# Two of the three layer-2 projections as seven block products, the ones products later, and the check of the sums in two parts

## The chip, the cores and the metric

The kernel runs on one core of one Trainium2 chip. The metric is the time of one execution on the device in microseconds (us). The core works with engines that run side by side and wait for each other through semaphores: TensorE (PE in the profile; its weight loads are PEld), VectorE (DVE), ScalarE (ACT), GpSimd (POOL) and the queue that starts most transfers (SP). A tile framework orders the instructions of each engine by its own schedule, so the order on an engine is not always that of the source.

## The reference

Eight images of 512 channels and 32 x 32 = 1024 pixels pass through four layers in float32, each layer on the output of the one before:

```python
# layer 0: 1x1 convolutions f, g, h (512 -> 64), z = f.T g per image, attn = z / sigma_max(z), x = x + Wv (attn h)
# layer 1, an attention over the 1024 pixels of an image with 512 channels:
h = _group_norm(x, gamma, beta).reshape(B, C, N)
q, k, v = wq h + bq, wk h + bk, wv h + bv
attn = softmax(q.T k * 512 ** -0.5)
x = x + wp (attn v) + bp
# layer 2, an attention with 128 channels:
proj = jnp.einsum('oc,ncq->noq', W_w, xf) + W_b[None, :, None]     # W_w: 384 x 512
t, p, g = jnp.split(proj, 3, axis=1)                                # 128 rows each
s = softmax(jnp.einsum('ncq,nck->nqk', t, p) * 128 ** -0.5, axis=2)
att = jnp.einsum('nqv,ncv->ncq', s, g)
x = x + batchnorm(Z_w att)
# layer 3: binarised 1x1 convolution, batchnorm, residual, PReLU
```

The changed part is t and p of layer 2: two matrices of 128 x 1024 per image, each a product of 128 x 512 weights with the image.

## The kernel before

A first part (about 210 us) loads and prepares weights, runs layer 0's convolutions and starts its singular values. Then `fast` runs once per image for layers 1 to 3; the singular values of later images (`chore`, `chain`) and the next image's products (`fill`) are put between the products of the current one. Tiles: P = 128, N = 1024, HF = 512, C = 512, CC = 4 channel blocks, NH = 2 halves of the pixels, NT = 8 and NTH = 4 pixel blocks, B = 8 images.

Large products are made from seven block products instead of eight (Strassen's scheme in Winograd's form). `sums_of` makes S1 to S4 from the blocks of the left matrix, `differences_of` T1 to T4 from those of the right one, and `seven` runs the products and adds them up. `product_of` gives `term`: two matmuls of 512 columns (or four of 256) for one block product.

```python
    def differences_of(b, more):

        b11, b12, b21, b22 = b
        t1, t2, t4 = more
        tt = nc.vector.tensor_tensor
        tt(t1, b12, b11, ALU.subtract)
        tt(t2, b22, t1, ALU.subtract)
        tt(b12, b22, b12, ALU.subtract)
        tt(t4, b21, t2, ALU.subtract)
        return {"B11": b11, "B21": b21, "B22": b22, "T1": t1, "T2": t2, "T3": b12, "T4": t4}

    def seven(term, c11, c12, c21, c22, b1=None, b2=None, exp=None, then=None):
        ...   # move: ScalarE PSUM -> SBUF with bias; plus: VectorE dst = PSUM (+ bias) + u
        pa, va = term(None, "A11", "B11", True, False)
        nc.scalar.copy(c21, va)
        yield
        _, vb = term(None, "S2", "T2", True, True)
        plus(vb, None, c21, c21)
        yield
        pd, vd = term(None, "S3", "T3", True, False)
        plus(vd, None, c21, c22)
        yield
        pc, vc = term(None, "S1", "T1", True, False)
        move(c12, vc, b2)
        nc.gpsimd.tensor_tensor(c22, c22, c12, ALU.add)
        yield
        term(pa, "A12", "B21", False, True)      # accumulates into the bank of A11 B11
        ...                                      # c11 <- va
        yield
        term(pc, "S4", "B22", False, True)
        plus(vc, b1, c21, c12)
        yield
        term(pd, "A22", "T4", False, True)
        plus(vd, b2, c21, c21)
        ...
```

`make_v` runs `seven` twice and `scores1` four times per image. Layer 2's t, p and g were made directly, and the row sums of the exponentials are turned into their inverses by `inverse_sums`, whose matmuls have a matrix of ones as weights:

```python
    def project2(env, xt, fill=lambda h: None):

        big = env["big"]
        tpg = big.tile([P, 3, N], F32, tag="us", name="tpg")
        tt, pt = tpg[:, 0:1, :], tpg[:, 1:2, :]
        gt = tpg[:, 2, :].rearrange("p (t c) -> p t c", c=P)
        for h in reversed(range(NH)):
            for i, dst in enumerate((tt, pt)):
                ps = bank()
                for cc in range(CC):
                    mm(
                        out=ps,
                        lhsT=sbw["tpg"][:, cc, bass.ts(i, P)],
                        rhs=xt[:, cc, half(h)],
                        start=cc == 0,
                        stop=cc == CC - 1,
                    )
                evacuate(i, dst[:, 0, half(h)], ps, col("L2_conv_W_b", i))
                fill(h)
            ps = bank().rearrange("p (t c) -> p t c", c=P)
            for i in range(4):
                for cc in range(CC):
                    mm(
                        out=ps[:, i, :],
                        lhsT=xt[:, cc, bass.ts(4 * h + i, P)],
                        rhs=sbw["tpg"][:, cc, 2 * P : 3 * P],
                        start=cc == 0,
                        stop=cc == CC - 1,
                    )
            nc.vector.tensor_tensor(
                gt[:, bass.ts(h, 4), :], ps, bg_row.unsqueeze(1).to_broadcast([P, 4, P]), ALU.add
            )
            fill(h)
        return tt, pt, gt

    def inverse_sums(env, esum, row):
        ps = bank()
        for h in range(NH):
            mm(out=ps[side(h), :], lhsT=ones2[:, 0:MID], rhs=esum[:, half(h)], start=True, stop=True)
        r = env["small"].tile([P, HF], F32, tag="rsum", name="rsum", bufs=1)
        nc.vector.reciprocal(r, ps)
        full = env["small"].tile([P, NH, HF], F32, tag="rfull", name="rfull", bufs=1)
        ...   # four DMAs: r to both halves of the partitions of full; two DMAs: rows of r to guard
        return full
```

The end of layer 1 (`values1`) updates the image `xt` in place on GpSimd, a half of a channel block at a time:

```python
        def scaled(dst, oc, h):               # inside values1
            nc.vector.tensor_tensor(dst, dst, r[:, h, :], ALU.mult)
            xs = xt[:, oc, half(h)]
            nc.gpsimd.tensor_tensor(xs, xs, dst, ALU.add)
        ...
        for i in range(2):
            group(pc[i], a12, e22, i, False, True)
            d = temp(i)
            tt(d, pc[i], u[i], ALU.add)
            scaled(d, i, 1)
            yield
        pd = [bank(), bank()]
        for i in range(2):
            group(pd[i], a21, e12, i, True, False)
            tt(p5[i], p5[i], u[i], ALU.add)
            tt(p5[i], pd[i], p5[i], ALU.add)
            scaled(p5[i], 2 + i, 1)
            yield
        for i in range(2):
            group(pd[i], a22, e21, i, False, True)
            tt(u[i], pd[i], u[i], ALU.add)
            scaled(u[i], 2 + i, 0)
            yield
```

One image, and the check of the row sums at the end of the last one (its result decides whether a general path runs after the fast one; with these inputs it does not):

```python
    def fast(env, n, hb, ua):
        ...                                   # scores1: seven products for each of 4 row blocks
        esum = es.pop()
        vt = env["big"].tile([P, NT, C], F32, tag="uv", name="vt")
        r = None
        for _ in make_v(hb, vt):              # 2 x seven products
            if r is None:
                r = inverse_sums(env, esum, n)
            chore(2)
        ...
        for k, _ in enumerate(values1(env, xt, vt, es, r, scratch)):   # 14 groups of 4 products
            ...                               # k == 5: h and its differences for the next image
        ...
        def fill(k=1):                        # one of the next image's u products
            for _ in range(k):
                next(steps, None)

        tt, pt, gt = project2(env, xt, lambda h: fill(1 - h))
        es, esum = scores2(env, pt, tt, lambda t: fill(t % 2))
        ...
        fill()
        values2(0, range(0, 1))
        r = inverse_sums(env, esum, B + n)
        values2(0, range(1, NTH))
        att = values2(0, range(NTH, NT))
        values2(1, range(0, NTH))
        close2(xt, att, 0)
        att = values2(1, range(NTH, NT))
        fill()
        for _ in leave(env, xt, dst, [0], signs):
            fill()
        close2(xt, att, 1)
        fill(2)
        for _ in steps:
            pass
        rest3.append(leave(env, xt, dst, [1], signs))
        if not more:                          # the last image
            verdict.append(count_bad(env))
            for _ in rest3.pop():
                pass

    def count_bad(env):
        g = 2 * B * 4
        ...                                   # tiles fine, other, nbad in the pool late
        nc.vector.tensor_scalar(fine, guard, 1.0 / GUARD, None, ALU.is_gt)
        nc.vector.tensor_scalar(other, guard, GUARD, None, ALU.is_lt)
        nc.vector.tensor_tensor(fine, fine, other, ALU.mult)
        ...                                   # twice: compare halves of guard, multiply into fine
        nc.vector.tensor_reduce(nbad, fine.rearrange("p h n -> p (h n)"), AX.X, ALU.min)
        nc.vector.tensor_scalar(nbad, nbad, -1.0, 1.0, ALU.mult, ALU.add)
        ps = bank()
        mm(out=ps[0:1, 0:1], lhsT=nbad, rhs=ones2[0:g, 0:1], start=True, stop=True)
        nc.vector.tensor_copy(bad, ps[0:1, 0:1])
        return nc.values_load(bad, min_val=0, max_val=P)
```

Of the kernel before, what the change touches and what calls it, by code (L numbers as in the profile page):

```python
# [83 lines left out]
def kernel(  # L84
# [527 lines left out]
    def project2(env, xt, fill=lambda h: None):  # L612

        big = env["big"]
        tpg = big.tile([P, 3, N], F32, tag="us", name="tpg")
        tt, pt = tpg[:, 0:1, :], tpg[:, 1:2, :]
        gt = tpg[:, 2, :].rearrange("p (t c) -> p t c", c=P)
        for h in reversed(range(NH)):
            for i, dst in enumerate((tt, pt)):
                ps = bank()  # L620
                for cc in range(CC):
                    mm(  # L622
                        out=ps,
                        lhsT=sbw["tpg"][:, cc, bass.ts(i, P)],
                        rhs=xt[:, cc, half(h)],
                        start=cc == 0,
                        stop=cc == CC - 1,
                    )
# [90 lines left out]
    def count_bad(env):  # L719
# [4 lines left out]
        fine = late.tile([g, NH, P], F32, tag="fine", name="fine")  # L724
        other = late.tile([g, NH, P], F32, tag="other", name="other")
# [14 lines left out]
        nc.vector.tensor_copy(bad, ps[0:1, 0:1])  # L740
        return nc.values_load(bad, min_val=0, max_val=P)
# [72 lines left out]
    def fast(env, n, hb, ua):  # L814
# [52 lines left out]
        tt, pt, gt = project2(env, xt, lambda h: fill(1 - h))  # L867
# [23 lines left out]
        values2(0, range(0, 1))  # L891
        r = inverse_sums(env, esum, B + n)
        values2(0, range(1, NTH))
# [3 lines left out]
        att = values2(1, range(NTH, NT))  # L897
        fill()
# [449 lines left out]
    with ExitStack() as main:  # L1348
# [9 lines left out]
        ua = got[0]  # L1358
        for n in range(B):
            hb, ua = fast(env, n, hb, ua)  # L1360
# [31 lines left out]
    def general(env, xt, b, dst):  # L1392
# [55 lines left out]
        tt, pt, gt = project2(env, xt)  # L1448
# [23 lines left out]
    with tc.If(verdict[0] > 0):  # L1472
        with (
            ExitStack() as stack,
            tc.tile_pool(name="gbig", bufs=1) as big,
            tc.tile_pool(name="gepool", bufs=2) as epool,
# [5 lines left out]
            for a in weights.values():  # L1482
                nc.vector.tensor_tensor(a["S3"], a["A11"], a["S3"], ALU.subtract)
# [45 lines left out]
```

## Time and profile before

Three executions took 1985.38, 1987.02 and 1988.73 us, median 1987.02. The profiled one has a span of 1984.6 us and a mean granted TensorE clock of 0.992.

| engine | busy us | share of the span | instructions |
|---|---|---|---|
| PE (matmuls) | 1929.4 | 97% | 6262 |
| PEld (weight loads) | 993.9 | 50% | 6262 |
| DVE | 1104.4 | 56% | 1807 |
| ACT | 507.8 | 26% | 803 |
| POOL | 203.9 | 10% | 168 |

A float32 matmul shows as two records in the trace, so counts of matmuls are twice those of the source: `project2`'s t and p have 16 matmuls of 512 columns per image, 128 in all, and 256 records. Records overlap in a pipeline: one lasts 592 ns for 512 columns, but the next one starts 429 ns after it when nothing holds it up. So a stream of matmuls is best measured from start to start. The timeline gives for each engine start, duration, line, tiles, count, and in brackets the idle time before it and who ended it. The groups by line and the waits give the same by kind, summed over the run.

### The profile page before, as it was taken

To read this page: it belongs to the slowest core of one execution; us is meant where nothing else is said; L and a number is where in the kernel's file an instruction comes from. 1 tells how busy PE (TensorE), PEld (TensorE's weight loads), DVE (VectorE), ACT (ScalarE), POOL (GpSimd) and SP (SyncE) were. 2 spreads that over 40 slices of the span, in tenths; PEclk is the share of its full clock that TensorE was granted. 3 is DMA by queue.
4 is the path that set the end of the run, shared out by engine and by line. 5 is a ranking of instruction groups with operands and counts; after the bars stand their busy time and mean duration, and the time that the engine had idled before them with its cause. 6 is when DMAs were issued, how large, how long until landed. Compare 5 with 4: busy or idle time off the path is not lost.

```text
span 1984.6 us, 16624 instructions
## 1 busy us (share of the span) xinstructions
PE 1929.4 (97%) x6262; PEld 993.9 (50%) x6262; DVE 1104.4 (56%) x1807; ACT 507.8 (26%) x803; POOL 203.9 (10%) x168
## 2 busy tenths in 40 slices
PE   8999899999999999999999999999999999999997
PEld 2377346544565446454455446444645445544653
DVE  3235577337863586536752677238653775266526
ACT  2132122034220432024211341034202421134114
POOL 1000101100011000200111002100120011101110
PEclk9989999999999999999999999999999999999999
DMA  8320000002000020001100120002000110010001
GB/s 332 128 75 1 6 6 12 1 11 85 11 6 0 22 74 17 0 0 57 45 11 1 32 69 11 0 11 85 11 0 1 54 44 9 0 32 22 11 1 55
DMA packets 26712, 66.99 MB, mean 34 GB/s; under 512 B 3760, under 2 KB 4016, under 8 KB 25984
## 3 DMA queue, kind: packets, MB, share of 16 engines
q1 hardware_dynamic: 25968, 65.09, 9.7%
q8 instruction: 51, 0.84, 0.2%
q0 software_dynamic: 224, 0.33, 0.1%
q10 hardware_dynamic: 432, 0.43, 0.1%
q14 instruction: 37, 0.30, 0.1%
HBM read 38.51 MB, written 18.87 MB: 29 GB/s over the span
## 4 chain that ended last, share of the span: by engine, by line
PE 92%; DVE 5%; ACT 2%; POOL 1%; issue 1%; DMA 0%; DVEq 0%; ACTq 0%
PE bank L370 36%; PE bank L537 19%; PE bank L875 6%; PE bank L622 6%; PE bank L755 6%; PE bank L1122 4%; PE bank L634 3%; PE bank L651 3%; PE bank L393 2%; PE bank L671 1%; PE bank L926 1%; PE bank L1232 1%; PE wide L1178 1%; PE bank L927 1%; PE bank L776 1%; DVE e L327 1%
## 5 line engine op out<-in xcount | busy, mean ns | idle before, releaser
L537 PE MATMUL bank<-e,vt 128*128 128x512 f32 x768 | 334.0, 593 | 0.0
L537 PEld LDWEIGHTS bank<-e,vt 128*128 128x128 f32 x768 | 145.0, 190 | 175.3 <-issue 171.7
L370 PE MATMUL bank<-ut,h 128*128 128x512 f32 x384 | 183.3, 598 | 4.7 <-ACT e L332 4.7
L370 PE MATMUL bank<-us,hs 128*128 128x512 f32 x256 | 121.3, 596 | 0.5 <-DVE us L299 0.5
L327 DVE TENSOR_TENSOR e<-bank,e 128x512 f32<-128x512 f32 x128 | 87.8, 686 | 61.1 <-PE bank L370 59.8
L875 PE MATMUL bank<-e,tpg 128*128 128x512 f32 x256 | 114.6, 595 | 0.0
L755 PE MATMUL bank<-tpg 128*128 128x512 f32 x256 | 114.6, 592 | 0.0
L370 PEld LDWEIGHTS bank<-ut,h 128*128 128x128 f32 x384 | 70.6, 190 | 87.7 <-issue 73.5
L622 PE MATMUL bank<-xt,tpg 128*128 128x512 f32 x256 | 113.6, 592 | 0.0
L762 ACT ACTIVATE e<-bank 128x512 f32<-128x512 f32 x128 | 76.4, 597 | 96.1 <-PE bank L755 96.1
L370 PE MATMUL bank<-wo,h 128*128 128x256 f32 x384 | 92.1, 383 | 5.6 <-ACT vt L332 5.6
L370 PE MATMUL bank<-h,wu 128*128 128x512 f32 x192 | 92.0, 602 | 4.7 <-DVE h L443 4.1
L327 DVE TENSOR_TENSOR vt<-bank,vt 128x512 f32<-128x512 f32 x64 | 43.9, 686 | 83.6 <-PE bank L370 82.7
L767 DVE TENSOR_TENSOR esum<-esum,e 128x1024 f32<-128x1024 f32 x48 | 58.8, 1225 | 54.9 <-ACT e L762 54.9
L342 POOL TENSOR_TENSOR e<-e 128x512 f32<-128x512 f32 x32 | 41.6, 1300 | 432.2 <-ACT e L321 361.3
L370 PEld LDWEIGHTS bank<-wo,h 128*128 128x128 f32 x384 | 71.6, 190 | 18.2 <-ACT vt L332 8.8
L875 PEld LDWEIGHTS bank<-e,tpg 128*128 128x128 f32 x256 | 48.0, 190 | 63.9 <-issue 63.9
L755 PEld LDWEIGHTS bank<-tpg 128*128 128x128 f32 x256 | 48.6, 190 | 60.7 <-issue 58.6
L342 POOL TENSOR_TENSOR ut<-ut 128x512 f32<-128x512 f32 x16 | 21.7, 1359 | 532.2 <-ACT ut L323 532.2
L622 PEld LDWEIGHTS bank<-xt,tpg 128*128 128x128 f32 x256 | 47.9, 190 | 56.4 <-issue 55.0
L370 PEld LDWEIGHTS bank<-us,hs 128*128 128x128 f32 x256 | 47.3, 190 | 57.5 <-issue 51.4
L661 ACT ACTIVATE sg<-xt,rb 128x512 f16<-128x512 f32 x64 | 43.7, 717 | 103.6 <-DVE xt L653 100.9
(304 smaller groups left out, 2974.3 us busy)
## 6 DMA issues: line engine op xcount, KB each, us to landing
xt<-in_x SPq DMA_DIRECT2D x56, 512.0 KB
out<-both SPq DMA_DIRECT2D x64, 256.0 KB
rfull<-rsum SPq DMA_DIRECT2D x64, 128.0 KB
f_dram<-f SPq DMA_DIRECT2D x8, 256.0 KB
fb<-f_dram SPq DMA_DIRECT2D x8, 256.0 KB
w<-in_w SPq DMA_DIRECT2D x1, 1024.0 KB
q<-in_w_q SPq DMA_DIRECT2D x1, 1024.0 KB
k<-in_w_k SPq DMA_DIRECT2D x1, 1024.0 KB
```

The source lines that it names most:

```text
L327: nc.vector.tensor_tensor(dst, ps, u, ALU.add)
L342: nc.gpsimd.tensor_tensor(c22, c22, c12, ALU.add)
L370: mm(out=ps[:, q * w : (q + 1) * w], lhsT=lt(ka, kb, q, k), rhs=rhs(ka, kb, q, k), start=first and q == 0 and k == 0, stop=last and k == 1 ...
L537: mm(out=ps, lhsT=a[:, t, bass.ts(r_, P)], rhs=e[t], start=first and t == 0, stop=last and t == NTH - 1, skip_group_check=True,)
L622: mm(out=ps, lhsT=sbw["tpg"][:, cc, bass.ts(i, P)], rhs=xt[:, cc, half(h)], start=cc == 0, stop=cc == CC - 1,)
L634: mm(out=ps[:, i, :], lhsT=xt[:, cc, bass.ts(4 * h + i, P)], rhs=sbw["tpg"][:, cc, 2 * P : 3 * P], start=cc == 0, stop=cc == CC - 1,)
L651: mm(out=ps, lhsT=sbw["z"][:, bass.ts(oc, P)], rhs=att, start=True, stop=True)
L755: mm(out=ps, lhsT=pt[:, 0, bass.ts(t, P)], rhs=tt[:, 0, half(h)], start=True, stop=True,)
L762: nc.scalar.activation(e[:, half(h)], ps, AF.Exp, scale=float(P) ** -0.5)
L767: nc.vector.tensor_tensor(esum, esum, e, ALU.add)
L875: mm(out=banks[h], lhsT=gt[:, t, :], rhs=es[t][:, half(h)], start=t == 0, stop=t == NT - 1,)
L1122: mm(out=banks[i][side(h), :], lhsT=w0[i][:, cc, :], rhs=xt[:, cc, half(h)], start=cc == 0, stop=cc == CC - 1,)
```

## The change

Three things change.

1. t and p become one product of 256 x 512 weights with the 512 x 1024 image, split in 2 x 2 blocks of 128 x 256 and 256 x 512, and made by `seven`. The weights' sums are formed once (`sp`, three tiles of 128 x 256, and one block of the weights overwritten). The differences are formed per image on VectorE from `xt`, each 128 x 1024, into four tiles of the pool `e` that also holds the exponentials; `xt` itself must stay, so `differences_of` takes a fourth tile. g stays direct and now comes after all of t and p; the next image's products are called at the last three steps.
2. The ones products of layer 1 come after the fourth product of `make_v` instead of after the first, and those of layer 2 after two of the value matmuls instead of one.
3. `count_bad` is a generator: its VectorE part is called before the output of the last image's first half, its matmul and the load of the result while the second half is put out. Two of its tiles move to another pool.

The aim is fewer matmuls, and ones products that do not hold up TensorE while the sums are still being formed. The diff (the general path's part, which does not run here, is cut, as are two changes of pool):

```diff
@@ -304,13 +304,13 @@
     def differences_of(b, more):
 
         b11, b12, b21, b22 = b
-        t1, t2, t4 = more
+        t1, t2, t4, t3 = (list(more) + [b12])[:4]
         tt = nc.vector.tensor_tensor
         tt(t1, b12, b11, ALU.subtract)
         tt(t2, b22, t1, ALU.subtract)
-        tt(b12, b22, b12, ALU.subtract)
+        tt(t3, b22, b12, ALU.subtract)
         tt(t4, b21, t2, ALU.subtract)
-        return {"B11": b11, "B21": b21, "B22": b22, "T1": t1, "T2": t2, "T3": b12, "T4": t4}
+        return {"B11": b11, "B21": b21, "B22": b22, "T1": t1, "T2": t2, "T3": t3, "T4": t4}
 
     def seven(term, c11, c12, c21, c22, b1=None, b2=None, exp=None, then=None):
 
@@ -609,25 +609,29 @@
             scaled(u[i], 2 + i, 0)
             yield
 
-    def project2(env, xt, fill=lambda h: None):
+    def project2(env, xt, made):
+
 
         big = env["big"]
         tpg = big.tile([P, 3, N], F32, tag="us", name="tpg")
         tt, pt = tpg[:, 0:1, :], tpg[:, 1:2, :]
         gt = tpg[:, 2, :].rearrange("p (t c) -> p t c", c=P)
+        wa = weights["tp"]
+        xb = differences_of(
+            [xt[:, chunks[k], half(n)] for k in range(2) for n in range(2)],
+            [env["e"].tile([P, 2, HF], F32, tag="e", name="xd") for i in range(4)],
+        )
+        term = product_of(lambda a, b, q, k: wa[a][:, k, :], lambda a, b, q, k: xb[b][:, k, :])
+        yield from seven(
+            term,
+            tt[:, 0, half(0)],
+            tt[:, 0, half(1)],
+            pt[:, 0, half(0)],
+            pt[:, 0, half(1)],
+            col("L2_conv_W_b", 0),
+            col("L2_conv_W_b", 1),
+        )
         for h in reversed(range(NH)):
-            for i, dst in enumerate((tt, pt)):
-                ps = bank()
-                for cc in range(CC):
-                    mm(
-                        out=ps,
-                        lhsT=sbw["tpg"][:, cc, bass.ts(i, P)],
-                        rhs=xt[:, cc, half(h)],
-                        start=cc == 0,
-                        stop=cc == CC - 1,
-                    )
-                evacuate(i, dst[:, 0, half(h)], ps, col("L2_conv_W_b", i))
-                fill(h)
             ps = bank().rearrange("p (t c) -> p t c", c=P)
             for i in range(4):
                 for cc in range(CC):
@@ -641,8 +645,8 @@
             nc.vector.tensor_tensor(
                 gt[:, bass.ts(h, 4), :], ps, bg_row.unsqueeze(1).to_broadcast([P, 4, P]), ALU.add
             )
-            fill(h)
-        return tt, pt, gt
+            yield
+        made.extend((tt, pt, gt))
 
     def close2(xt, att, h):
 
...
@@ -735,10 +739,12 @@
             nc.vector.tensor_tensor(fine[one, h, :], fine[one, h, :], other[one, h, :], ALU.mult)
         nc.vector.tensor_reduce(nbad, fine.rearrange("p h n -> p (h n)"), AX.X, ALU.min)
         nc.vector.tensor_scalar(nbad, nbad, -1.0, 1.0, ALU.mult, ALU.add)
+        yield
         ps = bank()
         mm(out=ps[0:1, 0:1], lhsT=nbad, rhs=ones2[0:g, 0:1], start=True, stop=True)
         nc.vector.tensor_copy(bad, ps[0:1, 0:1])
-        return nc.values_load(bad, min_val=0, max_val=P)
+        verdict.append(nc.values_load(bad, min_val=0, max_val=P))
+        yield
 
     def channels(ap):
         return ap.rearrange("(cc p) n -> p cc n", p=P)
@@ -841,9 +847,8 @@
             pass
         esum = es.pop()
         vt = env["big"].tile([P, NT, C], F32, tag="uv", name="vt")
-        r = None
-        for _ in make_v(hb, vt):
-            if r is None:
+        for k, _ in enumerate(make_v(hb, vt)):
+            if k == 3:
                 r = inverse_sums(env, esum, n)
             chore(2)
         scratch = env["big"].tile([P, 3, N], F32, tag="us", name="scratch")
@@ -864,7 +869,10 @@
             for _ in range(k):
                 next(steps, None)
 
-        tt, pt, gt = project2(env, xt, lambda h: fill(1 - h))
+        made = []
+        for k, _ in enumerate(project2(env, xt, made)):
+            fill(k > 5)
+        tt, pt, gt = made
         es, esum = scores2(env, pt, tt, lambda t: fill(t % 2))
         banks, r = [None, None], None
 
@@ -888,13 +896,15 @@
 
         dst = channels(out[b])
         fill()
-        values2(0, range(0, 1))
+        values2(0, range(0, 2))
         r = inverse_sums(env, esum, B + n)
-        values2(0, range(1, NTH))
+        values2(0, range(2, NTH))
         att = values2(0, range(NTH, NT))
         values2(1, range(0, NTH))
         close2(xt, att, 0)
         att = values2(1, range(NTH, NT))
+        count = iter(()) if more else count_bad(env)
+        next(count, None)
         fill()
         for _ in leave(env, xt, dst, [0], signs):
             fill()
@@ -904,9 +914,8 @@
             pass
         rest3.append(leave(env, xt, dst, [1], signs))
         if not more:
-            verdict.append(count_bad(env))
             for _ in rest3.pop():
-                pass
+                next(count, None)
 
         return hb, got[0] if more else None
 
@@ -1356,6 +1365,9 @@
         for _ in make_u(env, hb, got):
             pass
         ua = got[0]
+        sp = late.tile([P, 3, 2, P], F32, tag="sp", name="sp")
+        tp = quarters_of(sbw["tpg"], chunks, [slice(0, P), slice(P, 2 * P)])
+        weights["tp"] = sums_of(tp, [sp[:, i] for i in range(3)])
         for n in range(B):
             hb, ua = fast(env, n, hb, ua)
 
...
...
```

More of the change, by code (lines that the diff above doesn't have):

```diff
@@ L723, in count_bad @@
         g = 2 * B * 4
-        fine = late.tile([g, NH, P], F32, tag="fine", name="fine")
-        other = late.tile([g, NH, P], F32, tag="other", name="other")
+        fine = env["small"].tile([g, NH, P], F32, tag="half_a", name="fine")
+        other = env["small"].tile([g, NH, P], F32, tag="half_b", name="other")
         nbad = late.tile([g, 1], F32, tag="nbad", name="nbad")
@@ L1447, in general @@
         attention(env, rows1, float(C) ** -0.5, apply1)
-        tt, pt, gt = project2(env, xt)
+        made = []
+        for _ in project2(env, xt, made):
+            pass
+        tt, pt, gt = made
         def rows2(ps, t):
@@ L1475 @@
             tc.tile_pool(name="gbig", bufs=1) as big,
-            tc.tile_pool(name="gepool", bufs=2) as epool,
+            tc.tile_pool(name="gepool", bufs=4) as epool,
             tc.tile_pool(name="gsmall", bufs=2) as small,
@@ L1480 @@
             psum_pools(stack, 2, 4)
-            for a in weights.values():
+            for a in (weights["u"], weights["o"]):
                 nc.vector.tensor_tensor(a["S3"], a["A11"], a["S3"], ALU.subtract)
```

## The prediction

> **What bounds the kernel now.** I read the page's busy times first, then its chain that ended last, then the waits of TensorE, then the timeline of TensorE around the two places that the change touches, and last the timeline of the tail.
>
> ```profile
> PE 1929.4 (97%) x6262; PEld 993.9 (50%) x6262; DVE 1104.4 (56%) x1807; ACT 507.8 (26%) x803; POOL 203.9 (10%) x168
> ...
> PE 92%; DVE 5%; ACT 2%; POOL 1%; issue 1%; DMA 0%; DVEq 0%; ACTq 0%
> ```
>
> TensorE carries 92% of the chain that ended last. So a matmul removed is time gained nearly one for one, and work added to VectorE (56% busy) costs only where TensorE, or the short tail after it, waits for it. Where TensorE waits already is in the waits of that engine (line, releaser, us in total, times, longest):
>
> ```profile
> PE bank L776 <- DVE esum L517: 6.2, 7, 1.5
> PE bank L370 <- ACT vt L332: 5.6, 8, 0.7
> ...
> PE bank L370 <- DVE h L443: 4.1, 1, 4.1
> ```
>
> The first two belong together. L776 is the ones product of layer 1, which waits for the last addition to the row sums; the other is a product of `make_v`. The timeline of TensorE at one image (start, duration, what) shows both:
>
> ```profile
> 982.00 1.97 PE L370 MATMUL bank<-wo,h 128*128 128x256 f32 x8
> 984.64 1.99 PE L370 MATMUL bank<-wo,h 128*128 128x256 f32 x8 [0.67 <-ACT vt L332]
> 987.09 1.08 PE L776 MATMUL bank<-esum,ones 128*64 128x512 f32 x4 [0.46 <-DVE esum L517]
> 988.10 1.99 PE L370 MATMUL bank<-so,hs 128*128 128x256 f32 x8
> 989.93 1.89 PE L370 MATMUL bank<-wo,h 128*128 128x256 f32 x8
> 991.66 1.89 PE L370 MATMUL bank<-so,hs 128*128 128x256 f32 x8
> ```
>
> A block product undisturbed takes 1.72 us from start to start (991.66 - 989.93 = 1.73). The first one here takes 2.64, the second 2.45. The order explains it: the framework put A12 B21 directly after A11 B11, because the ones product stood next in the source and its operand wasn't there. A12 B21 accumulates into the bank that ScalarE has first to copy out, so it waits, and then the ones product waits for its sums all the same.
>
> The t and p products and their surroundings, from the timeline of TensorE and of VectorE and GpSimd at the same image:
>
> ```profile
> 1029.60 27.63 PE L537 MATMUL bank<-e,vt 128*128 128x512 f32 x64
> 1057.07 7.03 PE L622 MATMUL bank<-xt,tpg 128*128 128x512 f32 x16
> 1063.94 3.73 PE L634 MATMUL bank<-tpg,xt 128*128 128x128 f32 x32
> ...
> 1057.27 0.69 DVE L608 TENSOR_TENSOR o_a<-bank,o_a 128x512 f32<-128x512 f32 x1 [2.01 <-PE bank L537]
> ...
> 1048.47 1.27 POOL L550 TENSOR_TENSOR xt<-xt,o_b 128x512 f32<-128x512 f32 x1 [2.10 <-DVE o_b L548]
> 1051.90 1.27 POOL L550 TENSOR_TENSOR xt<-xt,o_b 128x512 f32<-128x512 f32 x1 [2.17 <-DVE o_b L548]
> 1055.34 1.27 POOL L550 TENSOR_TENSOR xt<-xt,o_a 128x512 f32<-128x512 f32 x1 [2.17 <-DVE o_a L548]
> 1058.77 1.27 POOL L550 TENSOR_TENSOR xt<-xt,o_a 128x512 f32<-128x512 f32 x1 [2.17 <-DVE o_a L548]
> ```
>
> Half of t and p (8 matmuls, 16 records) runs from 1057.07 to 1063.94, with no wait: 6.87 / 8 = 0.859 us a matmul. VectorE is idle two thirds of this stretch. The four POOL lines are the last updates of `xt`: channel blocks 2 and 3 of the right half, then of the left half, the last one done at 1060.04, 3 us after the products of layer 2 have begun.
>
> [...]the GpSimd addition of L576 takes 1262 ns at best and 2248 in the median, beside VectorE's L581[...].
>
> **The change part by part.**
>
> *Fewer matmuls.* Per image t and p take 2 x 2 x 4 = 16 matmuls of 512 columns; seven block products of two matmuls take 14. Two times 0.859 us times 8 images is 13.7 us less, all of it on the chain. g keeps its 32 short matmuls; the number of products of the next image that fill in stays three.
>
> *Do the new operands come in time?* The four differences take 1.22 us each on VectorE, 4.9 us per image. I follow them by hand at the image shown. T1 needs the left and right halves of blocks 0 and 1 and a buffer whose exponentials are read by the first matmuls after 1046.8; it can run from 1048.4 to 1049.6[...]. T2 and T3 need the addition that ends at 1053.2 (or 1053.8): T2 at 54.5 to 55.0, T3 at 55.7 to 56.2. That pushes L608 and its multiplication at the left half of block 2 by some 2 us, and the last addition by up to 1, to 1061.0. T4 follows to 1062.3. TensorE: A11 B11 at 1057.1, S2 T2 at 1058.8 (T2 is there 4 us before), S3 T3 at 1060.5, S1 T1 at 1062.2, A12 B21 at 1063.9 (its last input 3 us before), S4 B22 at 1065.7, A22 T4 at 1067.4 (T4 5 us before). No wait. The sums afterwards (four VectorE, three ScalarE, one GpSimd operation instead of two and two) end about 1 us after A22 T4, and the first reader, the scores, comes only after 7 us of g and 5 of fillers. In the built order of the changed kernel the 14 matmuls do stand in this order, with g behind them. So VectorE's added time, 6 us per image, costs nothing here.
>
> *Ones later.* In the built order `make_v` now begins A11 B11, S2 T2, S3 T3, S1 T1, ones, A12 B21: ScalarE has 5 us for its copy, and the sums, which were ready at 987.0, are read at 982.0 + 4 x 1.72 = 988.9. Both waits go: 5.6 + 6.2 = 11.8 us of idle time. Each stop also loses the overlap of two records, since the idle time is counted from the modelled end (0.38 us for 256 columns) and not from the pitch (0.215): 15 stops x 0.165 = 2.5 us. Together 14.3; I take 14.0, should one or another leave a trace. The inverses now come 1.7 us later, but they are first used 20 us on. In layer 2 no wait of L776 for L767 stands among TensorE's waits, so the shift there gains nothing; the value matmuls behind it, 10 instead of 11 before the next reader, still cover the reciprocal (3.36), the transfer (3.03) and the multiplication (0.69).
>
> *Weights' sums.* Four VectorE operations of 128 x 256, 0.42 us each and 0.33 from start to start. They stand in the built order among the small operations that lead to the first h, which TensorE awaits in the 4.1 us wait above. The first fills a wait for GpSimd, three lie on the path: + 1.0 us, once.
>
> *The check in two parts.* At the end VectorE is the bound:
>
> ```profile
> 1962.29 2.48 DVE L690 SCALAR_TENSOR_TENSOR both<-bank,sa,xt 128x512 f32<-128x512 f32 x3 [0.17 <-PE bank L671]
> 1964.74 0.75 DVE L702 SCALAR_TENSOR_TENSOR both<-up,ps,both 128x512 f32<-128x512 f32 x1
> ...
> 1970.58 0.13 DVE L740 CAST bad<-bank 1x1 int32<-1x1 f32 x1
> ```
>
> From 1962.3 to 1970.7 it has no rest, and the last signs of the second half wait for it. In the kernel before, the check's small operations run at 1956.0 to 1960.2, in a gap. In the built order of the changed kernel all but the first lie between the steps of this busy stretch: 0.20 + 0.33 + 0.40 + 0.50 + 0.45 + 0.10 = 2.0 us, of which the first fits before L690. I count + 1.7 us. Against it, TensorE no longer meets the check's matmul ahead of the signs (a stop of about 0.2), which does not decide the end.
>
> Sum: 1987.0 - 13.7 - 14.0 + 1.0 + 1.7 = 1962.0. For waits that I have not seen I add 1: 1963 us.
>
> **The rivals.** First: the products of layer 2 come to wait for the differences. The old ones needed only `xt`; the new ones need a chain of GpSimd, VectorE and a free buffer. For it speaks [...]that VectorE executes in order, so that T4's wait for the last addition holds up whatever stands behind it. Against it speak 3 to 5 us of margin at every product. If it were so at one product per image, by 1 us, the gain would be 8 us smaller: 1971. Second: the seven products hold more banks and put three stops into accumulations, as in `make_v` before, where A12 B21 waited 0.67 us for a copy. Here three products lie between, so I don't expect it; it would cost 8 x 0.9 = 7 us. Third: the ones product is only held up elsewhere, for instance because the later reciprocal (3.36 us) delays the additions of `make_v`'s second half. VectorE has gaps of 3.1, 2.8 and 4.6 us there, so I give it little. With it half of the 14 would stay: 1970. Fourth: the tail loses nothing, since ScalarE has work to catch up there; then 1961.
>
> **Range and chances.** The matmuls are sure to half a us, the ones to about 2, tail and start to 1.5 together; the three rivals that cost are each unlikely and partial. The three times of before spread over 3.4 us. I take 1957 to 1970. Faster by 2% would need 1947.3, below every sum here, as no more than 28 us of waits and matmuls are touched; slower by 2% would need a stop of 8 us at every image. Faster 0.02, within 2% 0.96, slower 0.02.
>
> **What the profile after would show.** 224 records of the t and p products instead of 256, without idle time before them; no wait of TensorE for `vt` at L332 and none for the sums in layer 1; VectorE's busy time up by about 50 us to 1155, TensorE's down by about 14; the wait for the first h longer by about 1 us; the last stretch from the last layer-2 value product to the end longer by 1 to 2 us. I would be wrong if TensorE shows a new wait for `xd` or for `xt` at GpSimd in each image, or if the stops in `make_v` only change their name.

## The result, and the profile after

| | median us | lowest to highest | runs |
|---|---|---|---|
| before | 1987.85 | 1985.38 to 1988.73 | 4 |
| after | 1958.74 | 1958.62 to 1959.65 | 4 |

The ratio is 0.986 (95% interval 0.984 to 0.987): 28 us less, between 25 and 32. The prediction said 1963 and a range of 1957 to 1970. The runs of one kernel differ by up to 4.3 us (the split check alone, below). In the traces, one per kernel, most of what differs without a part of the change behind it lies ahead of the first `make_v` product: the first u product starts at 210.03 to 212.05 us in the three kernels that do the same work up to there, and the first `make_v` product 88.65 to 89.62 us later. Behind that, stretches repeat to 0.02 us, except the last one, from the first z product of the last image to the end, which repeats to 0.3 us. So the parts of the change are compared below by stretches of the trace and not by the times alone.

The page's busy times and shares of the chain of the kernel after:

```profile
PE 1913.9 (98%) x6230; PEld 989.2 (51%) x6230; DVE 1151.2 (59%) x1859; ACT 512.8 (26%) x811; POOL 223.9 (11%) x176
...
PE 93%; DVE 3%; ACT 2%; DMA 0%; issue 0%; POOL 0%; DVEq 0%; ACTq 0%
```

TensorE has 15.5 us less to do, VectorE 46.8 us more, and the bound is the same engine. The waits of TensorE after (line, releaser, us in total, times, longest):

```profile
PE bank L1131 <- DMA fg<-in_w_fg: 5.3, 1, 5.3
PE bank L370 <- DVE h L443: 4.9, 1, 4.9
PE bank L370 <- ACT e L332: 4.7, 7, 0.7
PE bank L935 <- DVE cur L957: 3.9, 3, 1.8
PE bank L420 <- DVE dev L417: 2.5, 1, 2.5
```

The two groups that stood first before, 6.2 us for the row sums and 5.6 us for the copy into `vt`, are gone; no wait for `xd` has come. The first line belongs to the start and was there before (5.4 us). The seven waits of 0.7 us for the copy into `e` were there before too, and come back below. `make_v` of the image that the prediction showed, in the timeline of TensorE and of VectorE after:

```profile
970.94 1.97 PE L370 MATMUL bank<-wo,h 128*128 128x256 f32 x8
...
972.75 1.89 PE L370 MATMUL bank<-so,hs 128*128 128x256 f32 x8
...
974.48 1.89 PE L370 MATMUL bank<-wo,h 128*128 128x256 f32 x8
...
974.76 1.22 DVE L517 TENSOR_TENSOR esum<-esum,e 128x1024 f32<-128x1024 f32 x1
...
976.21 1.89 PE L370 MATMUL bank<-so,hs 128*128 128x256 f32 x8
...
978.03 1.08 PE L782 MATMUL bank<-esum,ones 128*64 128x512 f32 x4
```

Behind the first, the products follow each other at 1.73 us, the sums end at 975.98, and the ones product reads them 2 us later. The t and p products of the same image, with the VectorE and GpSimd work that feeds them:

```profile
1035.71 1.22 DVE L309 TENSOR_TENSOR xd<-xt 128x1024 f32<-128x1024 f32 x1
1035.87 2.18 POOL L550 TENSOR_TENSOR xt<-xt,o_b 128x512 f32<-128x512 f32 x1 [2.10 <-DVE o_b L548]
...
1039.30 1.26 POOL L550 TENSOR_TENSOR xt<-xt,o_b 128x512 f32<-128x512 f32 x1 [1.26 <-DVE o_b L548]
1040.60 1.23 DVE L310 TENSOR_TENSOR xd<-xt,xd 128x1024 f32<-128x1024 f32 x1 [1.38 <-POOL xt L550]
...
1044.47 1.88 PE L370 MATMUL bank<-xt,tpg 128*128 128x512 f32 x4
...
1046.19 1.88 PE L370 MATMUL bank<-xd,sp 128*128 128x512 f32 x4
1046.26 1.27 POOL L550 TENSOR_TENSOR xt<-xt,o_a 128x512 f32<-128x512 f32 x1 [0.63 <-DVE o_a L548]
...
1047.56 1.23 DVE L312 TENSOR_TENSOR xd<-xt,xd 128x1024 f32<-128x1024 f32 x1 [1.38 <-POOL xt L550]
1047.91 1.88 PE L370 MATMUL bank<-xd,tpg 128*128 128x512 f32 x4
...
1051.34 1.88 PE L370 MATMUL bank<-xt,tpg 128*128 128x512 f32 x4
...
1054.77 1.88 PE L370 MATMUL bank<-xd,tpg 128*128 128x512 f32 x4
```

The seven products (S1 T1 and S4 B22 are among the lines left out) start every 1.72 us, none with idle time in brackets, which would name what was waited for. L310 is T2, the addition at 1046.26 the last to `xt`, L312 T4. T2 ends at 1041.83, 4.4 us ahead of S2 T2; the last addition to `xt` at 1047.53, 3.8 us ahead of A12 B21; T4 at 1048.79, 6.0 us ahead of A22 T4. The prediction's hand timeline had 4, 3 and 5.

### The profile page after: what moved, and what is told of

The parts are those of the page before. It is cut to its first block, busy times and chain, and to the rows that moved or that the text cites. A ratio compares the mean times of both kernels' runs of the same rounds, so it can differ in the third digit from the quotient of the medians.

```text
span 1957.9 us, 16696 instructions
## 1 busy us (share of the span) xinstructions
PE 1913.9 (98%) x6230; PEld 989.2 (51%) x6230; DVE 1151.2 (59%) x1859; ACT 512.8 (26%) x811; POOL 223.9 (11%) x176
## 4 chain that ended last, share of the span: by engine, by line
PE 93%; DVE 3%; ACT 2%; DMA 0%; issue 0%; POOL 0%; DVEq 0%; ACTq 0%
PE bank L370 43%; PE bank L537 20%; PE bank L883 6%; PE bank L761 6%; PE bank L1131 4%; PE bank L638 3%; PE bank L655 3%; PE bank L393 2%; PE bank L675 1%; PE bank L935 1%; PE wide L1187 1%; PE bank L1241 1%; PE bank L936 1%; PE bank L782 1%; PE quad L1044 1%; ACT both L699 0%
## 5 line engine op out<-in xcount | busy, mean ns | idle before, releaser
L790 DVE RECIPROCAL rsum<-bank 128x512 f32<-128x512 f32 x16 | 53.7, 3355 | 30.3 <-PE bank L782 30.3
L1131 PE MATMUL bank<-xt,fg 128*64 128x512 f32 x256 | 58.6, 608 | 5.3 <-DMA fg<-in_w_fg 5.3
```

Source lines behind the costliest of these rows:

```text
L1131: mm(out=banks[i][side(h), :], lhsT=w0[i][:, cc, :], rhs=xt[:, cc, half(h)], start=cc == 0, stop=cc == CC - 1,)
```

## The experiments

To see which part brought what, I took TensorE's start times at fixed places of the program (first u product, first `make_v` product, first layer-2 score, first z product of each image, end) and subtracted those of the kernel before. In us, from the traces:

| stretch | after | products alone | ones alone | check alone |
|---|---|---|---|---|
| start to the first `make_v` | +1.90 | +0.96 | +2.28 | +0.27 |
| `make_v`, images 1 to 3, each | -2.59 | 0 | -2.59 | 0 |
| `make_v`, images 4 to 7, each | -1.54 | 0 | -1.54 | 0 |
| `make_v`, image 8 | -1.02 | 0 | -1.02 | 0 |
| t, p and g, each image | -1.72 | -1.72 | 0 | 0 |
| first z product of the last image to the end | +0.15 | +2.86 | -0.25 | +0.62 |

All runs of the study, against runs of the kernel before that were taken alongside (medians 1986.5 to 1986.8 us):

| run | median us | lowest to highest | ratio (95%) |
|---|---|---|---|
| e1_tp, products alone | 1977.24 | 1976.39 to 1977.96 | 0.995 (0.994 to 0.997) |
| e2_ones, ones later alone | 1971.79 | 1970.56 to 1973.35 | 0.992 (0.991 to 0.994) |
| e3_count, split check alone | 1989.56 | 1986.85 to 1991.18 | 1.001 (1.000 to 1.002) |
| e4_diff2, differences twice | 1960.04 | 1959.69 to 1960.12 | 0.986 (0.985 to 0.988) |
| e5_diff3, differences three times | 2016.20 | 2015.77 to 2017.22 | 1.015 (1.013 to 1.017) |
| e6_k2, ones one place earlier | 1959.60 | 1959.29 to 1959.94 | 0.986 (0.985 to 0.988) |
| e7_unsplit, check in one piece | 1961.39 | 1960.88 to 1962.15 | 0.987 (0.986 to 0.989) |
| b5_swap, z products later | 1954.29 | 1954.16 to 1954.54 | 0.984 (0.982 to 0.985) |
| b8_early, check further up | 1958.21 | 1957.65 to 1958.23 | 0.986 (0.984 to 0.987) |
| b7_all, both (and the sums' place in the source) | 1953.32 | 1953.12 to 1955.29 | 0.983 (0.982 to 0.985) |

### The products alone

The ones and the check go back to their old places in the source; the check's two tiles stay where the change put them.

```diff
-            if k == 3:
+            if k == 0:
                 r = inverse_sums(env, esum, n)
...
-        count = iter(()) if more else count_bad(env)
-        next(count, None)
...
+            for _ in count_bad(env):
+                pass
             for _ in rest3.pop():
-                next(count, None)
+                pass
```

> The kernel before with the t and p products of layer 2 alone: seven block products in place of eight times two full ones, the weights' sums formed ahead of the first image, four more difference buffers; the ones products and the check of the sums stand as before. My theory: two matmuls of 0.859 us fewer in each of 8 images, -13.7 us, and the weights' sums on the way to the first h, +0.8 us: about 1974 us against 1987 before, with both stops of make_v (the copy into vt, the row sums) still in the trace, some 12 us of idle time of TensorE. Rival: the four new VectorE differences, 6 us per image with their additions, are paid in part; then 1978 to 1985 and a wait of TensorE for the differences or for xt in each image.

It came out at 1977.2, 9 us under before and not 13. The table tells why: each image gains 1.72 us, exactly two matmuls (8 x 1.716 = 13.7), and the end loses 2.86. The waits of TensorE in this run:

```profile
PE bank L782 <- DVE esum L517: 6.1, 7, 1.5
PE bank L370 <- ACT vt L332: 5.6, 8, 0.7
...
PE bank L744 <- DVE nbad L741: 4.6, 1, 4.6
```

The first two are the old stops of `make_v`, as expected, and no wait for the differences stands here: the rival falls. The third is new, and neither theory had it. The timeline of the end of this run shows where it comes from:

```profile
1948.43 3.62 PE L675 MATMUL bank<-sg,signs 128*128 128x512 f16 x16
1949.24 0.27 DVE L732 TENSOR_SCALAR other<-guard 64x256 f32<-64x256 f32 x1
...
1957.78 0.28 DVE L731 TENSOR_SCALAR fine<-guard 64x256 f32<-64x256 f32 x1
...
1960.11 0.19 PE L744 MATMUL bank<-ones,nbad 64*1 64x1 f32 x2 [4.63 <-DVE nbad L741]
...
1960.23 5.27 PE L675 MATMUL bank<-sg,signs 128*128 128x512 f16 x16
```

One operation of the check runs at 1949, the other 8.5 us later. Its tile `fine` now takes turns with `up3`, the buffer of the output step, and in the source it stands behind the first half's outputs. TensorE, in order, waits for the check's tiny matmul ahead of the signs of the second half. And those 16 records then take 5.27 us, where the same ones of the first half took 3.62 (the first line): after the stop the granted clock is 0.68 (from 1960.1 to 1965.5, by the view of stretches) against 1.00. That the tile's buffer is the reason was read here from the source and the timeline; the kernel with the check in one piece, below, was forecast from it.

### The ones products alone

```diff
-        r = None
-        for _ in make_v(hb, vt):
-            if r is None:
+        for k, _ in enumerate(make_v(hb, vt)):
+            if k == 3:
                 r = inverse_sums(env, esum, n)
...
-        values2(0, range(0, 1))
+        values2(0, range(0, 2))
```

> The kernel before with the ones products later alone (behind the fourth product of make_v in layer 1, behind the second value matmul in layer 2). My theory: the two stops of make_v go, -14 to -15 us, about 1972.5 us; by image the same stretch as in the changed kernel, 2.6 us shorter in images 1 to 3, 1.5 in images 4 to 7, 1.0 in the last. Rival: the stop is only held up elsewhere, half stays: about 1980. If the parts of the change help each other, this and the products alone add up to less than the whole, -28 us.

1971.8, that is 14.8 less than before, and all of it in `make_v`: 3 x 2.59 + 4 x 1.54 + 1.02 = 14.95 in the trace. Neither wait is left among TensorE's. The shift in layer 2 moves the ones by 0.86 us and nothing behind them. This run and the one before add up to -24 us, the whole gives -28. In the traces 2.5 us of these 4 lie at the end of the program, where the products alone meet the stop for `nbad`; the rest is no more than the starts differ by. So the products and the ones do not help each other; the split helps the products, as the next runs show.

### The check of the sums in two parts

To the kernel before, with its t, p and ones as they were:

```diff
-        fine = late.tile([g, NH, P], F32, tag="fine", name="fine")
+        fine = env["small"].tile([g, NH, P], F32, tag="half_a", name="fine")
...                                                   # other likewise, half_b
+        yield                                        # behind the last operation on nbad
...
         att = values2(1, range(NTH, NT))
+        count = iter(()) if more else count_bad(env)
+        next(count, None)
         fill()
```

> The kernel before with the check of the sums in two parts alone. Prediction on record: the five small VectorE operations stand between the steps of the last stretch, which VectorE bounds: +1.7 us at the end, about 1988.7. Rival (the fourth one on record): VectorE ends later by less than 1 us and the end after it is shorter by as much, since the check's matmul no longer stands in front of the signs: 0.0 to +0.3, 1987.

All starts stay as they were (within 0.04 us behind the first `make_v`) up to the first z product of the last image; from there to the end it takes 0.62 us more. VectorE's last output operation comes 25.67 us after that product, where it was 24.76 before: +0.92. In the changed kernel it is 25.67 too, so this is what the split costs VectorE in both; what follows that operation took 5.43, 5.14 and 4.67 us in before, here and after. So the prediction's 1.7 is too much, and 0.0 to 0.3 too little. The median is 3 us above before: five of the twelve runs took 1986.9 to 1987.2 us, seven 1989.5 to 1991.2. The traced run is one of the five, so what lengthened the seven is not shown.

The other side of the split, the changed kernel with the check in one piece:

```diff
         att = values2(1, range(NTH, NT))
-        count = iter(()) if more else count_bad(env)
-        next(count, None)
         fill()
```

> The changed kernel with the check of the sums in one piece as before, its tiles staying in the pool that the change moved them to. My theory from the products alone: one of those tiles takes turns with the buffer of the output step, so that in one piece the check waits for the first half's outputs, and TensorE for it, 4.6 us ahead of the second half's signs: VectorE's last operation 2.6 us later than in the changed kernel, 1961.3. Rival (the prediction's term taken alone): without the split VectorE's last stretch loses the check's 0.9 to 1.7 us again: 1957 to 1958.

1961.4, as expected: 4.62 us of wait of TensorE for `nbad` again, and the last stretch 2.41 us longer than in the changed kernel. So the split is no loss in this change. With the tiles moved, the split is what keeps the check from stopping TensorE; against the kernel before, tiles and split together delay VectorE's last operation by 0.92 us and lengthen the last stretch by 0.15 (after) and 0.62 us (the split alone), where that stretch varies by 0.3. The block products with the tiles in their old place weren't tried, so why they moved stays open.

Where the 0.9 lies can be tested by moving the first part further up, ahead of the last value product:

```diff
         close2(xt, att, 0)
+        count = iter(()) if more else count_bad(env)
+        next(count, None)
         att = values2(1, range(NTH, NT))
-        count = iter(()) if more else count_bad(env)
-        next(count, None)
```

> The changed kernel with the first part of the check two lines further up, ahead of the last product of the last batch's second attention half. In the built order its small VectorE operations now stand before the multiplication of that half, in the 5 us in which VectorE waits for TensorE, instead of between the steps of the output. My theory: the 0.9 us that the split in its present place costs the last stretch is gained back, 1957.8; the prediction's 1.7 would make it 1957.0. Rival: the end is set by the write of the last output, which varied between 4.7 and 5.4 us after VectorE's last operation in the traces so far, and nothing is seen in the time.

The timelines of VectorE at this place, first after, then with the check further up:

```profile
1935.20 0.27 DVE L732 TENSOR_SCALAR other<-guard 64x256 f32<-64x256 f32 x1
1935.46 0.75 DVE L694 SCALAR_TENSOR_TENSOR both<-bank,sa,xt 128x512 f32<-128x512 f32 x1
1936.13 0.41 DVE L733 TENSOR_TENSOR fine<-fine,other 64x256 f32<-64x256 f32 x1
1936.46 0.73 DVE L694 SCALAR_TENSOR_TENSOR both<-bank,sa,xt 128x512 f32<-128x512 f32 x1
```

```profile
1932.41 0.15 DVE L741 TENSOR_SCALAR nbad<-nbad 64x1 f32<-64x1 f32 x1
1933.88 0.69 DVE L892 TENSOR_TENSOR att<-bank,rfull 128x512 f32<-128x512 f32 x1 [1.32 <-PE bank L883]
1934.74 1.61 DVE L694 SCALAR_TENSOR_TENSOR both<-bank,sa,xt 128x512 f32<-128x512 f32 x2 [0.17 <-PE bank L675]
```

In the second all of the check is done before the multiplication that VectorE waits for, and the output steps stand together. VectorE's last operation comes 24.75 us after the first z product, as in the kernel before, so the 0.92 us are gained back. The stretch to the end is 0.78 us shorter. The rival, that the end hides it, falls in the trace; in the times alone, 0.5 us between medians that were not taken alongside each other, it can't be told.

### How much margin the differences have

Each difference is formed two or three times, with the same result:

```diff
-        tt = nc.vector.tensor_tensor
+        def tt(*a):
+            for _ in range(2 if len(more) == 4 else 1):     # 3 in the second run
+                nc.vector.tensor_tensor(*a)
```

> The changed kernel with each of the four differences of layer 2 formed twice (same result, written twice): 32 more VectorE operations of 1.22 us, +39 us of VectorE's busy time. My theory: the differences have 3 to 5 us of margin, so TensorE's next product is never held up by 2.4 us more: 0 to +2 us against the changed kernel, 1958.7 to 1960.7, and no wait of TensorE for the differences. Rival: the margins are an artefact of my hand timeline and each us of VectorE before these products costs: T2 or T3 is late by 1 to 2 us in each image, +8 to +16.

1960.0: VectorE is busy 44 us longer and the time rises by 1.3 us. In the trace one stop shows, for T3 in the second image (0.79 us of wait, 1.02 of time); the end is 0.29 us longer, which is within what that stretch varies by. In the image shown the last addition to `xt` now ends at 1050.76, and A12 B21 starts at 1051.42: of the 3.8 us 0.7 are left.

> The changed kernel with each difference formed three times: 64 more VectorE operations of 1.22 us, +78 us busy, 9.8 us more ahead of the products in each image. My theory: twice was free but for one stop of 1 us, so the margin of 3 to 5 us is now used up: T3 and T4 are late by about 1 us each where the framework leaves the products in place; +2 us in each image, +10 to +16 in all, about 1971, with a wait of TensorE for xd in each image. Rival one: the margin is larger than I worked out and it stays at 1959 to 1961. Rival two: VectorE's order (the scaling of the last outputs behind the differences) is what holds TensorE, through xt: then the wait is for xt and grows by the full 4.9 us of an image, +35.

This missed: 2016.2, +57 us, more than my 10 to 16 and than either rival. The waits of TensorE (all lines stand 3 further down in this kernel):

```profile
PE bank L373 <- DVE xd L310: 19.8, 16, 3.6
PE bank L373 <- POOL xt L553: 15.6, 7, 2.2
```

So 35 us are waits, for both operands. I had moved T3 and T4 alone and forgotten that VectorE works through its instructions in order: the eight extra operations also delay the multiplications ahead of the last additions to `xt`, and with them B21. That is the second rival's path; its size was too small, since the wait for `xd` comes on top. An image has 8 x 1.14 us more (1.14 from start to start), less 3.8 of margin is 5.3; the fifth and seventh images lose 5.72 each. The other images lose 6.3 to 8.4, and most of the rest of the 57 us is this, in the timeline of the fourth:

```profile
1068.31 1.98 PE L373 MATMUL bank<-xd,sp 128*128 128x512 f32 x4 [1.23 <-DVE xd L310]
1070.13 1.02 PE L373 MATMUL bank<-xt,tpg 128*128 128x512 f32 x2
1073.38 2.08 PE L373 MATMUL bank<-xt,tpg 128*128 128x512 f32 x2 [2.22 <-POOL xt L553]
1075.77 3.78 PE L373 MATMUL bank<-xd,tpg 128*128 128x512 f32 x4 [0.32 <-DVE xd L310]
1079.35 2.27 PE L373 MATMUL bank<-xd,sp 128*128 128x512 f32 x4
1081.45 1.02 PE L373 MATMUL bank<-h,wu 128*128 128x512 f32 x2
```

Four records took 1.88 us in the lines of after and take 3.78 here. The same run by stretches (length, then the busy time of TensorE's matmuls; the granted clock is the number behind the last count in brackets):

```profile
1069.88:1073.29 3.41, 1.28 (x3) 0.21 (x2) 2.32 (x3) 0.00 (x0) 2.14 (x1) 1.00 0.00 0
1073.29:1076.70 3.41, 3.00 (x3) 1.00 (x4) 3.34 (x3) 0.69 (x1) 0.03 (x1) 0.50 0.03 5
1076.70:1080.12 3.42, 3.42 (x5) 1.35 (x4) 2.42 (x4) 0.00 (x0) 0.00 (x0) 0.50 0.00 0
```

After two stops within 5 us the clock is at half for 6.8 us. Beyond the margin VectorE's time is paid as a wait, and in six of the eight images a second time, as slower matmuls behind the wait.

### The place of the ones products

```diff
-            if k == 3:
+            if k == 2:
                 r = inverse_sums(env, esum, n)
```

> The changed kernel with the ones products of layer 1 behind the third product of make_v instead of the fourth, one dose between before and after. By the trace of the changed kernel the row sums of a late image end at 975.98 while the place behind the third product is at 970.94 + 3 x 1.74 = 976.2. My theory: the stop that counted was the hoisted A12 B21 waiting for the copy, and the sums come just in time: 0 to +0.3 us an image, 1959 to 1961, no wait of TensorE for the copy into vt. Rival: the place of the ones product is what matters by itself, half the gain is lost: about +7, 1966.

1959.6. From the start of `make_v` to the layer-1 values it takes 0.2 us more than after in each of the first three images and as long as after (to 0.01) in the five later ones. No wait for the copy into `vt` is in its list. It isn't the place behind the fourth product that pays, but that a product whose operands are ready stands behind A11 B11, and that the sums are there.

### The same fault elsewhere

The waits of after still have seven of 0.7 us for the copy into `e`. They are at the start of `scores1`, in the timeline of after:

```profile
1124.94 1.88 PE L370 MATMUL bank<-ut,h 128*128 128x512 f32 x4
1127.49 1.13 PE L370 MATMUL bank<-ut,h 128*128 128x512 f32 x2 [0.68 <-ACT e L332]
1128.45 1.88 PE L370 MATMUL bank<-us,hs 128*128 128x512 f32 x4
```

The second line is A12 B21 behind A11 B11 again: the sums `us` of S2 T2 aren't formed yet, since the last u products have only just ended. The edit puts the z products between:

```diff
-        close2(xt, att, 1)
         fill(2)
         for _ in steps:
             pass
+        close2(xt, att, 1)
```

> The changed kernel with the z products of the second half behind the last u products of the next image instead of ahead of them. In the changed kernel the scores of layer 1 begin with the same fault that make_v had: A12 B21 stands directly behind A11 B11 and waits 0.68 us for a copy, since the sums of u for S2 T2 are not formed; 0.84 us from start to start in each of 7 images. My theory: with 3.4 us of z products in between the sums are there, A11 B11 is followed by S2 T2, and the stop goes: -5.9 us, about 1953. Rival: the z products come later, so do xt and the signs of the output step, and TensorE waits for those instead: 1957 to 1960.

1954.3, 4.4 less than after. The timeline of the same place:

```profile
1119.27 3.60 PE L655 MATMUL bank<-att,z 128*128 128x512 f32 x8
1122.70 1.88 PE L370 MATMUL bank<-ut,h 128*128 128x512 f32 x4
1124.53 1.98 PE L370 MATMUL bank<-us,hs 128*128 128x512 f32 x4
```

A11 B11 is followed by S2 T2, though 1.83 us later and not 1.72: `us` is finished at the same moment. So five of the seven images gain 0.73 instead of 0.84 us, the first two 0.57 and 0.58: 4.8 in the trace. No wait for the signs has grown.

> The changed kernel with both edits that paid: the z products behind the last u products (-4.4 us when alone) and the first part of the check further up (-0.9). They lie in different places, so I expect the sum: 1953.4, faster than the kernel before by 33 us. Rival: they meet in the last image and one of them is lost: 1954.3.

1953.3, as the sum said: 33 us under before, ratio 0.983 (0.982 to 0.985). In the trace the end is 0.87 us shorter than with the z products alone. This kernel has a third edit: the weights' sums stand in the source behind the first image's scores instead of ahead of that image. In the built order they did not move (207.40 to 210.03 us, in the same place of VectorE's order), and the wait for the first h is 4.9 us as in after, so it neither adds nor takes. This is the best kernel of the study.

## Why the prediction was right, step by step

*Fewer matmuls.* 13.7 was worked out, 8 x 1.716 = 13.73 measured, alone and in the whole. There are 8 x 28 = 224 records of t and p, none with a wait.

*Operands in time.* Right, with margins of 4.4, 3.8 and 6.0 us against 4, 3 and 5. Doubling the VectorE work used up most of the margin at almost no cost; trebling it broke it. So the step was right for a reason that can be counted, not because VectorE is free. The first rival (products that wait for the differences) and the second (accumulations that stop) fall.

*Ones later.* Predicted 14.0, measured 14.95, the same alone and in the whole. The term that was too small is what I had called the overlap that each stop loses: 14.95 less 11.8 us of listed idle time, over 15 stops, is 0.21 us a stop on average, where I had taken 0.165 from the difference of a record's modelled length and its pitch. The third rival (half of it held up elsewhere) falls.

*Weights' sums.* Predicted +1.0. The wait for the first h is 4.6 to 4.9 us in all kernels of the study that form the sums and 3.8 to 4.1 in the three that don't. From the last record of the tiny matmul ahead of it (L420) to the first u product it takes 4.31 us before and 5.11 after: 0.8 us, a little less than predicted.

*The check in two parts.* This is the one term that was clearly mis-sized: +1.7, from 2.0 us of small operations put between steps of a stretch in which VectorE "has no rest". They take 1.8 us of VectorE's time there, but its last output operation comes only 0.92 later, and the end 0.15 to 0.62. VectorE did have rest: in the kernel before the first three output operations start 0.82 us apart (the 2.45 us of x3 in the prediction's line), as they wait for TensorE's sign products, and 0.66 apart where nothing holds them up; with what it waits ahead of the first of them, some 0.7 of the 1.8 us fitted in. The fourth rival (the tail loses nothing) is nearer for the end alone, though not by its reason: the check further up gains 0.78 us there. And the prediction took the split for a cost put on its own, while the run without it shows what it is for: the moved tiles would stop TensorE for 4.6 us.

*One us for waits not seen* was not needed. Most of the 4 us by which 1963 was too high are three terms that erred in one direction: 1.0 of the ones, 1.6 of the check by the end, and this one. Sum with the measured terms: -13.7 - 14.95 + 0.8 + 0.15 = -27.7 us; the two traces lie 26.7 us apart, since the start in that of after is 1.1 us longer beyond the sums; the medians lie 29 apart, 28 by the ratio.

The lengths of single instructions hold after as well. A difference takes 1216 to 1226 ns, and one of the weights' sums 414 to 417. Two matmuls fewer came to 1.716 us, 858 ns each, where the prediction had 859. The GpSimd addition beside T1 at 1035.87 takes 2.18 us, and the ones at 1039.30 and 1046.26, which have no VectorE instruction beside them, 1.26 and 1.27.

## What to carry to other kernels

When an in-order engine takes a product out of turn and waits, look for the operand that the framework found missing, and put work with ready operands there; the same fault can stand at several places, and the waits' list names them by the copy they wait for. Count a margin for a slower engine through everything that stands behind the new work in its order, not only to the new result: here it cost almost nothing up to the margin (1.3 us for 44) and then its full time, and on TensorE more than its time. A tile that moves to a shared pool inherits the waits of the buffer's other users, so judge such a part of a change together with what keeps it out of their way.

## What the runs showed that I had not expected

TensorE fell to half its clock behind short stops, and only in some of the images. With the differences three times the mean granted clock is 0.983, where after has 0.991. In that run it fell to half in six of the eight images, once behind a pause of 3.63 us and otherwise behind pauses of at most 2.23. The fourth image's lines above are cut at the changes of the clock (1073.29 and 1080.12, 6.83 us apart) and at half that distance, 3.41 us. The stretch ahead of the fall has 3.41 less 1.28, that is 2.13 us without a matmul. In the fifth image, cut along the same steps, pauses of the same lengths lie differently: the two stretches have 1.93 and 1.57 us without a matmul, and the clock stays:

```profile
1288.33:1291.74 3.41, 1.48 (x4) 0.38 (x2) 2.53 (x3) 0.00 (x0) 1.93 (x1) 1.00 0.00 0
1291.74:1295.16 3.42, 1.85 (x4) 0.79 (x5) 3.14 (x3) 0.69 (x1) 0.24 (x1) 1.00 0.00 0
```

What decides between the two was not shown: no run moved the pauses on purpose.

The clock goes with a part of what the starts differ by, too. Ahead of the first `make_v` product, between 130 and 220 us, it is at half for 17.07 and 6.83 us in before (298.9 us to that product) and for 17.07 and 10.24 us in after (300.8): 3.41 us more, where the start of after is 1.1 us longer beyond the weights' sums.

A single stop of 4.6 us was followed by a mean of 0.68 over the next 5.4 us in the kernel with the products alone, and by 0.72 over 5.1 us in the one with the check in one piece.

The other point is the price of a stop: on average 0.21 us more than the idle time that the waits list, over the 15 stops that went. It isn't one figure for all: the stop at the start of `scores1` costs 0.84 us from start to start for 0.68 listed, 0.16 more.
